# Two convolution layers with generated weights: wider statistics of x, an earlier start, first weights made beside the last loads, stores mixed with loads, last batch merged late

## The chip, the cores and the metric

The kernel runs on one core of one Trainium2 chip. The metric is the device time of one execution in microseconds. Several executions are timed in rounds against the kernel before on the same chip. No slow state showed in any run. A program on one core has a state only where several runs agree, so the two single runs (e2, e3) are of unknown state, and they are used for their profiles.

## The reference, cut to what matters

Two layers of the same form. Each normalizes x in 32 groups along the last axis, makes a convolution kernel of its own for each of 32 batches and 256 positions from a small network on z, applies it, and adds a bias and x itself.

```python
# x: (32 samples, 32 batches, 64 channels, 256 positions), float32
h = relu(layernorm(z @ W1 + b1))            # hidden layer, 128 wide
w = (h @ W2 + b2).reshape(B, L, CI, CO, 3)  # a kernel for each batch and position
bias = relu(layernorm(z @ Wb1 + bb1)) @ Wb2 + bb2
out = einsum('sbilk,bliok->sbol', x_unfolded, w) + bias
x = x + out(groupnorm(x))                   # twice, with weights of its own each time
```

The second layer's normalization needs statistics of the whole output of the first. The first needs those of the whole input.

## The kernel before

The kernel works in **units**: unit v is half the output channels of one batch, 64 units a layer. In a unit TensorE makes 12 weight groups (16 matmuls each, line 383 and 384), VectorE and ScalarE take them into the tile `wall`, and then the product (four blocks, line 426) multiplies the normalized x in `xn` with them. VectorE adds the residual (line 436) and, in layer 0, takes statistics of the result (line 228). GpSimd normalizes (line 373) and adds the bias (line 350). SyncE issues nearly all transfers in one order.

```python
gmean = const.tile([P, G, S], FP, name="gmean")
rstd = const.tile([P, G, S], FP, name="rstd")
parts = const.tile([P, GT, B, NH, 6], FP, name="parts")
prep = const.tile([P, 3, GT], FP, name="prep")       # 96 bytes a partition
...
w2 = big.tile([P, C, K * C], FP, name="w2t")
xn = big.tile([P, 2, M + 2, S], FP, name="xn")
room = big.tile([P, SH * L + RING * CH * LT], FP, name="room")
ys = room[:, S * M :].rearrange("p (r o l) -> p r o l", r=RING, l=LT)   # residual ring
```

```python
def store(v):                       # after the product of unit v
    u, h = divmod(v, NH)
    if u < B:
        nc.sync.dma_start(out=x1[u][h], in_=residual(v))       # 1 MB in 8 KB rows
        for t in range(NT):
            for a in range(2):                                 # 8 stores, runs of 128 bytes
                nc.sync.dma_start(
                    out=x1p[u][a * C + h * CH : a * C + (h + 1) * CH, :,
                               t * MT : (t + 1) * MT].rearrange("o s m -> s o m"),
                    in_=residual(v)[t * S : (t + 1) * S, :, a * MT : (a + 1) * MT])
...
def after(v):
    u, h = divmod(v, NH)
    if v >= 0:
        store(v)
    if v + 2 < NH * U:
        load_residual(v + 2)
    ...                             # hidden layer of a later batch
    if v + 1 == NH * B:             # between the layers
        stats()
        for k in range(2):
            next_pairs(B, k)        # normalize half a batch, load the next
    w, k = (u + 1, 1) if h == 0 else (u + 2, 0)
    if w != B:
        next_pairs(w, k)
    if v + 1 < NH * U:
        add_bias(v + 1)
    if v + 2 < NH * U:
        load_bias(v + 2)            # 4 loads of 256 KB
```

The opening (not shown) streams x once for its statistics, 256 elements an instruction, beside the 32 steps of the small network.

## Time and profile before

| | before |
|---|---|
| time, median of 3 runs | 4169.68 us (4168.51 to 4170.45) |
| profiled span | 4157.9 us (this execution took 4159.7 us, 10 less than the median) |
| first product starts | 319.7 us |
| layer 0, product 0 to product 61 | 1874.0 us, 30.7 us a unit |
| boundary, product 61 to product 66 | 188.5 us |
| product 66 to the end (layer 1) | 1775.7 us, 28.8 us a unit |

The page and the stretches of this kernel are read in the prediction below. Three more readings carry the argument after it. First, layer 0's loop from product 1 to product 61, sixty units (columns: stretch and length; busy time of PE, TensorE's matmuls, PEld, its weight loads, DVE, which is VectorE, ACT, which is ScalarE, and POOL, which is GpSimd, each with its instruction count; granted TensorE clock as a share of full speed; share of the DMA engines' time in use; GB/s):

```profile
349.70:2193.70 1844.00, 1747.98 (x42245) 1695.60 (x42245) 1211.18 (x1440) 560.64 (x1920) 920.69 (x180) 1.00 0.66 176
```

Second, the waits in that stretch (engine and line, what was waited for: us in total, times, longest us). "issue" is time in which the engine waited for nothing that the profile shows:

```profile
PE pc L426 <- issue: 81.8, 108, 2.4
```

Third, the same kind of line for layer 1, from product 67 on:

```profile
PE pc L426 <- issue: 12.2, 27, 0.9
```

So the products of layer 0 lose 82 us to waits without a visible reason, and those of layer 1 hardly any (12 us). Layer 1 has the same matmuls; it has neither the small-run stores nor the statistics. The page's DMA section lists an instruction queue, 709 packets and 11.62 MB (16.4 KB each). The "instruction blocks" of the prediction and of the expectations are these packets.

### The profile page before, as it was taken

The numbers are of one execution on the slowest core, as the hardware profiler recorded it, in microseconds if no ns is written. First come the engines' busy times: TensorE is split into PE (matmuls) and PEld (weight loads), VectorE is DVE, ScalarE is ACT, GpSimd is POOL, SyncE is SP. The second block draws the span as 40 slices with busy tenths as digits, with TensorE's granted clock in tenths as the row PEclk, the third lists the DMA queues.
The fourth block names the chain that finished last, engine by engine and source line by source line (L and its number), as shares of the span: only waits on it lengthen the run. The fifth ranks groups of instructions, "written<-read, shape, count | busy, mean of one in ns | idle before, by whom it ended". The sixth has DMA issues, their size and how long they took to land.

```text
span 4157.9 us, 194021 instructions
## 1 busy us (share of the span) xinstructions
PE 3917.2 (94%) x90704; PEld 3741.3 (90%) x90704; DVE 2642.2 (64%) x3168; ACT 1306.7 (31%) x4296; POOL 2078.0 (50%) x618
## 2 busy tenths in 40 slices
PE   5879999999999999999997899999999999999999
PEld 3449999999999999999997899999999999999998
DVE  6876666666666666666666465565655656555565
ACT  3433332322323323223232233333333333333332
POOL 3446544554554454454450744555445554455542
PEclk8669999999999999999999999999999999999999
DMA  8966676666666666667667354454444444444442
GB/s 316 343 247 186 172 188 160 179 186 170 182 169 176 187 163 181 177 170 186 164 176 208 125 163 153 144 167 131 160 150 145 163 131 162 150 148 159 135 153 88
DMA packets 655151, 718.51 MB, mean 173 GB/s; under 512 B 568516, under 2 KB 584968, under 8 KB 586248
## 3 DMA queue, kind: packets, MB, share of 16 engines
q1 hardware_dynamic: 628232, 692.46, 56.2%
q8 instruction: 709, 11.62, 1.2%
q10 hardware_dynamic: 26112, 13.64, 1.1%
q14 instruction: 98, 0.80, 0.1%
HBM read 492.08 MB, written 213.91 MB: 170 GB/s over the span
## 4 chain that ended last, share of the span: by engine, by line
PE 85%; DVE 6%; issue 3%; POOL 2%; DMA 2%; ACT 1%; ACTq 0%; SPq 0%; POOLq 0%; DVEq 0%
PE pg L383 54%; PE pc L426 23%; PE pg L384 7%; DVE wall L394 3%; POOL sq L182 1%; DVE parts L228 1%; DVE room L436 1%; DMA bd<-bs 1%; POOL xn L373 1%; ACT ht L200 0%; ACT sq L174 0%; PE p L170 0%; DMA spare<-in_xs_dram 0%; DMA xn<-in_xs_dram 0%; DMA room<-in_xs_dram 0%
## 5 line engine op out<-in xcount | busy, mean ns | idle before, releaser
L383 PE MATMUL pg<-hT,w2t 128*64 128x128 f32 x24576 | 2726.4, 273 | 13.6 <-DVE wall L394 9.4
L384 PE MATMUL pg<-hT,w2t 128*64 128x128 f32 x24576 | 2726.0, 273 | 1.9 <-issue 1.8
L383 PEld LDWEIGHTS pg<-hT,w2t 128*64 128x64 f32 x24576 | 2677.8, 137 | 36.9 <-DVE wall L394 22.9
L384 PEld LDWEIGHTS pg<-hT,w2t 128*64 128x64 f32 x24576 | 2678.0, 137 | 3.8 <-issue 3.8
L394 DVE TENSOR_TENSOR wall<-pg,b 128x1024 f32<-128x1024 f32 (+1 forms) x1536 | 1865.6, 1220 | 689.5 <-PE pg L384 685.9
L409 ACT ACTIVATE wall<-pg,b 64x128 f32<-64x128 f32 x4096 | 1189.1, 486 | 2640.8 <-DVE wall L394 2109.5
L373 POOL TENSOR_TENSOR xn<-room,gmean 128x2048 f32<-128x2048 f32 x128 | 605.8, 4733 | 1768.7 <-PE pc L426 1703.0
L426 PE MATMUL pc<-wall,xn 128*32 128x128 f32 (+2 forms) x40960 | 986.3, 253 | 122.9 <-issue 105.8
L426 PEld LDWEIGHTS pc<-wall,xn 128*32 128x32 f32 x40960 | 934.7, 110 | 181.2 <-issue 164.1
L436 DVE TENSOR_TENSOR room<-pc,room 128x512 f32<-128x512 f32 x512 | 354.2, 692 | 751.0 <-PE pc L426 629.2
L373 POOL TENSOR_TENSOR xn<-xn,rstd 128x2048 f32<-128x2048 f32 x128 | 786.5, 6145 | 10.0
L350 POOL TENSOR_TENSOR room<-room,bt 128x2048 f32<-128x2048 f32 x128 | 591.1, 4618 | 85.9 <-DMA bt<-bd 61.3
L228 DVE BATCH_NORM_STATS2 parts<-room 128x6 f32<-128x256 f32 x672 | 246.4, 416 | 8.7
L182 POOL TENSOR_TENSOR sq<-sq 128x512 f32<-128x512 f32 (+2 forms) x192 | 104.0, 541 | 150.9 <-ACT sq L174 138.4
L170 PE MATMUL p<-wc,zt 17*128 17x256 f32 x256 | 89.6, 506 | 36.5 <-DMA zt<-in_L_conv_z_dram 36.5
L170 PEld LDWEIGHTS p<-wc,zt 17*128 17x128 f32 x256 | 61.4, 252 | 57.1 <-DVE parts L228 32.7
L197 PEld LDWEIGHTS p<-ident,hs 128*128 128x128 f32 x256 | 49.9, 222 | 51.4 <-issue 51.4
L210 PE MATMUL p<-ht,Wb 128*64 128x512 f32 x64 | 59.3, 1027 | 31.5 <-ACT ht L200 31.5
L197 PE MATMUL p<-ident,hs 128*128 128x128 f32 x256 | 61.6, 421 | 3.7 <-DVE hs L188 3.7
L228 DVE BATCH_NORM_STATS2 parts<-xn 128x6 f32<-128x256 f32 x192 | 64.0, 408 | 0.0
L228 DVE BATCH_NORM_STATS2 parts<-spare 128x6 f32<-128x256 f32 x160 | 53.5, 411 | 0.0
L210 PEld LDWEIGHTS p<-ht,Wb 128*64 128x64 f32 x64 | 8.4, 185 | 47.4 <-ACT ht L200 44.5
(43 smaller groups left out, 232.0 us busy)
## 6 DMA issues: line engine op xcount, KB each, us to landing
bt<-bd SPq DMA_DIRECT2D x512, 256.0 KB, 8.3
room<-in_xp_dram SPq DMA_DIRECT2D x64, 1024.0 KB, 9.7
room<-in_xs_dram SPq DMA_DIRECT2D x64, 1024.0 KB, 5.8
x<-room SPq DMA_DIRECT2D x64, 1024.0 KB, 4.2
x1p<-room SPq DMA_DIRECT2D x512, 128.0 KB, 4.4
room<-x1p SPq DMA_DIRECT2D x64, 1024.0 KB, 8.9
room<-x SPq DMA_DIRECT2D x64, 1024.0 KB, 8.2
out_dram<-room SPq DMA_DIRECT2D x64, 1024.0 KB, 4.8
```

The lines of the kernel that those rows point to most:

```text
L170: nc.tensor.matmul(self.p1[:, k], self.zt[:, k * P : (k + 1) * P], self.t["wc"], start=True, stop=True)
L182: nc.gpsimd.tensor_tensor(to, self.sq[:, :, 0:w], self.sq[:, :, w : 2 * w], ALU.add)
L197: nc.tensor.transpose(p2[:, net, k * P : (k + 1) * P], hs[:, 2 * k + net, :], ident)
L228: nc.vector.bn_stats(out, y.rearrange("p o (a m) -> p o a m", a=2)[:, :, :, g * e : (g + 1) * e])
L350: nc.gpsimd.tensor_tensor(y, y, bts.pop(v), ALU.add)
L373: nc.gpsimd.tensor_tensor(o, i, b, op)
L383: nc.tensor.matmul(pg[0:C, k, :], w[:, k0 * C : (k0 + 1) * C], h0, start=True, stop=True)
L384: nc.tensor.matmul(pg[C:P, k, :], w[:, k1 * C : (k1 + 1) * C], h1, start=True, stop=True)
L394: nc.vector.tensor_tensor(place(rows, a), pg[rows].rearrange("p o (t m) -> p t m o", t=NT), b2[n][rows, kind, None, None, o0 : o0 + OG].to ...
L409: nc.scalar.activation(place(rows, 0)[:, :, :, k], pg[rows, k].rearrange("p (t m) -> p t m", t=NT), AF.Identity, bias=b2[n][rows, kind, o0 ...
L426: nc.tensor.matmul(pc[t * S : (t + 1) * S, n0 - q * EB : n1 - q * EB, :], xn[:, u % 2, t * MT + p + 1, :], wall[:, t, a : a + (n1 - n0) * CH],
L436: nc.vector.tensor_tensor(part, pc.rearrange("p (m a) o -> p o a m", a=2), part, ALU.add)
```

## The change

Its parts, by what they intend:

1. Statistics of x over 512 elements, so 256 instructions instead of 512.
2. The x stream first in the queue, layer 0's small weights on ScalarE's queue, the network's scratch moved into `xn`, so that `wall` can lie in the big pool and take x meanwhile.
3. Nine of the first unit's twelve weight groups made beside the last x chunks; the first normalizing on VectorE.
4. At the boundary, the first 31 batches' statistics reduced one unit early, the last batch merged in with small instructions; the bias before, other normalizing behind.
5. The eight small-run stores issued 2, 1 and 5 at a time between the loads.

```diff
+    wall = big.tile([P, NT, WT], FP, name="wall")
-    prep = const.tile([P, 3, GT], FP, name="prep")
+    first_parts = parts.rearrange(...)[:, 0 : GT * B * 6]
+    prep = const.tile([P, 6, GT], FP, name="prep")
 ...
+            small = [load_small(stage, layers[0], 0, nc.scalar)]
             made = {0: Hidden(stage, zts, small, 0)}
+            load(1)
+            load(2)
+            small.append(load_small(stage, layers[1], 1, nc.sync))
 ...
+                if i == first - 2:
+                    for k in range(NL):
+                        center(stage, small[k], k)
+                if i == (NQ - 2) * SQ:
+                    first_weights()
-                bn_stats(parts[:, g, u, h, :], xv[q % NX][:, j], g)
+                bn_stats(first_parts[:, g, u, 0, :], xu[q][:, j], g)
 ...
             if v + 1 == NH * B:
-                stats()
-                for k in range(2):
-                    next_pairs(B, k)
+                store_pairs(v, range(8))
+                last_batch()
+                diagonals()
+                return
+            store_pairs(v, range(2))
             w, k = (u + 1, 1) if h == 0 else (u + 2, 0)
             if w != B:
                 next_pairs(w, k)
+            store_pairs(v, range(2, 3))
             if v + 1 < NH * U:
-                add_bias(v + 1)
-            if v + 2 < NH * U:
-                load_bias(v + 2)
+                next_bias(v + 1)          # add_bias(v + 1), load_bias(v + 2)
+            if v + 2 == NH * B:
+                next_bias(v + 2)
+            store_pairs(v, range(3, 8))
+            if v + 1 == NH * (B - 1):
+                batches(parts, B - 1)
 ... (cut: reductions split up, normalize_first, main loop)
```

One line looks like bookkeeping: `prep` grows from 3 rows to 6 for the merging. It is a 96-byte tile that becomes 192 bytes, and every tile allocated behind it moves.

## The prediction

> **What bounds the kernel now.** I read the page first (engine totals, then the slices), then stretches by engine, then the timelines of the opening and of the boundary between the layers. The engine totals and one group, from the page:
>
> ```profile
> PE 3917.2 (94%) x90704; PEld 3741.3 (90%) x90704; DVE 2642.2 (64%) x3168; ACT 1306.7 (31%) x4296; POOL 2078.0 (50%) x618
> ...
> L228 DVE BATCH_NORM_STATS2 parts<-room 128x6 f32<-128x256 f32 x672 | 246.4, 416 | 8.7
> ```
>
> TensorE is the bound overall, so only the places where it stands idle or half idle can give time. The stretches: opening, loop of layer 0, boundary, loop of layer 1 (columns: stretch and length, busy time of PE, PEld, DVE, ACT, POOL, granted clock, DMA share, GB/s):
>
> ```profile
> 27.00:277.00 250.00, 205.32 (x576) 119.67 (x576) 210.67 (x570) 110.87 (x192) 110.44 (x224) 0.69 0.93 344
> 320.00:2262.00 1942.00, 1837.72 (x44412) 1782.86 (x44404) 1271.85 (x1512) 587.86 (x2016) 957.27 (x188) 1.00 0.67 178
> 2262.00:2327.00 65.00, 37.43 (x827) 32.77 (x820) 31.39 (x37) 12.24 (x35) 37.68 (x8) 0.84 0.42 125
> 2327.00:4144.00 1817.00, 1799.15 (x44180) 1773.48 (x44180) 1091.53 (x1007) 581.50 (x2016) 940.11 (x185) 1.00 0.46 148
> ```
>
> Layer 0's loop has 104 us of TensorE idle (1942 - 1838), layer 1's 18. The first product is at 319.75 us; until then everything is opening. In the opening DMA (93%), TensorE (82%) and VectorE (84%) are all nearly full. TensorE's timeline there, four of its 32 steps of the small network:
>
> ```profile
> 45.40 3.78 PE L170 MATMUL p<-wc,zt 17*128 17x256 f32 x8
> ...
> 81.36 1.99 PE L170 MATMUL p<-wc,zt 17*128 17x256 f32 x8
> 84.69 1.97 PE L210 MATMUL p<-ht,Wb 128*64 128x512 f32 x2 [1.34 <-ACT ht L200]
> 86.59 1.76 PE L197 MATMUL p<-ident,hs 128*128 128x128 f32 x8
> 88.27 1.99 PE L170 MATMUL p<-wc,zt 17*128 17x256 f32 x8
> ```
>
> A step takes 6.9 us (81.36 to 88.27) when the first matmuls take 1.99, because TensorE then waits for ScalarE, whose own round is Square 1.02, GpSimd's seven additions 3.93, Sqrt 0.3, two Relu 1.43: about 6.8. When they take 3.78 the step is 7.5. Over the opening the mean is 7.3 us (211 us for 29 steps). The small network is a bound of its own. VectorE's timeline at the start:
>
> ```profile
> 18.58 0.41 DVE L142 TENSOR_REDUCE wm<-wc 17x2 f32<-17x256 f32 x1 [17.57 <-DMA wc<-in_L_conv_Wb_dram]
> ...
> 25.31 7.21 DVE L228 BATCH_NORM_STATS2 parts<-xn 128x6 f32<-128x256 f32 x22
> ...
> 42.16 1.23 DVE L188 TENSOR_TENSOR hs<-p,var 128x1024 f32<-128x1024 f32 x1
> ```
>
> A weight of 8 KB issued at 5.8 us came at 18.5, just after the 4 MB load issued before it on the same queue (5.14 to 18.04).
>
> [...] its instruction queue has 709 packets and 11.62 MB, 16.4 KB each, and layer 0's chain shows products run in pieces of about 120 to 128 matmul records (each with its weight load) with waits called "issue" between. [...] the 22 statistics above come every 328 ns (7.21/22).
>
> **The change, part by part.**
>
> 1. Statistics over 512 elements. 512 instructions of 328 ns (168 us) become 256 [...], but VectorE isn't the sole bound, so little of it shows.
>
> 2. Start. The x load is first in the queue, in four pieces, so statistics start near 10 us instead of 25. But VectorE centers the weights of both layers after only six statistics, and layer 1's weights are issued on the sync queue behind loads 0, 1 and 2: 12.6 MB at 375 GB/s is 34 us, so they come at about 38 us. VectorE stands until then, then does ten statistics (6 us), and the first network scaling comes at about 45 us (before: 42.16). The early start is lost.
>
> 3. The network is squeezed into 13 of 16 chunks of statistics. It has 5.9 long statistics per step instead of 15 short ones (3.5 us against 5), but the step's round is ScalarE and GpSimd [...], neither changed. With somewhat less DMA crowding I take 7.1 us: the second scaling at 51, the last (thirty later) at 51 + 213 = 264 us (before: 268.7). Then 9 + 16 + 16 statistics remain before the last chunk (24 us), and that chunk's load must wait for the network's last stores out of the same buffer (about 13 us after the last scaling, and then 13 us for 4 MB): statistics end at 264 + 26 + 10 = 300, against 277.5 before. **This costs 22 us.**
>
> 4. After the statistics. Before, 42 us went from their end to the first product: eight reduction steps (11 us), diagonals and spreading (8), then 12 weight groups (21) beside GpSimd's 21.5 us of normalizing and 4.7 of bias. Now nine groups are made by ScalarE, 3 x 16 + 6 x 8 = 96 activations at 284 ns (2.27/8), 27 us, from when chunk 13 is done (280) to 308; the shorter reductions (512 instead of 1024 elements, about 4.5 us) end at 305 beside it. Then diagonals and spreading 7, three groups to 320.5, sixteen normalizing instructions [...] on VectorE (10): first product at about 330 against 319.75. **Opening: +11 us.**
>
> 5. Last batch merged. Before, from the end of the last layer 0 product (2271) to the first of layer 1 (2326.8) are 55.5 us, with reductions of 11 us, a stand before the spreading, and GpSimd doing two halves (21.5), the next batch's half (10.7) and the bias (4.5) in that order. Now the 31 batches are reduced one unit earlier, only eleven tiny instructions (2.2 us) remain, the bias is added before and the next batch's half after. Spreading ends about 13 us after the products, normalizing on GpSimd 22 us later: 35 us, 20 less. The early reduction (five of 1.5 us) stops the taking of weight groups in its unit and, with three PSUM buffers, costs TensorE about 7. **Boundary: -13 us.**
>
> 6. Loads and small-run stores interleaved. The same 0.52 million packets of 128 B move, but five of eight stores of a half batch go after the bias load, so the last 5 us before and into the products carry small packets instead of big loads. No engine waits for these loads now; what it may touch is the 1.4 us of "issue" per unit in layer 0 (64 x 1.4 = 90 us). [...] traffic reaching further into the products works the other way. Estimate: a fifth of it, **-18 us**, the least certain term.
>
> Sum: 4169.7 + 11 - 13 - 18 = 4150.
>
> **Rivals.** (a) The opening gains: if layer 1's weights came early, scaling would start near 20 us and every later step with it, making the opening -14 instead of +11, total 4125. For: the change plainly intends it. Against: the 18.5 us landing above. (b) Instruction waits grow: stores now run to about 25 us after the start of a unit of 31 us, and the products start at 21; if a block waits as it did beside the last weight loads at 2264 us (2.9 us of issue), a unit loses 1 us more, total 4230. For: that wait; against: those were big packets. (c) The interleaving removes most issue waits: layer 0's unit falls from 31.0 to near 29.5, total 4080.
>
> **Range and chances.** The opening is good to 10 us either way, the boundary to 6, the loop to 30: together about 35. The change looks tuned, which shifts some weight to the fast side. I say 4150, 4100 to 4195, and faster by over 2% (under 4086) needs rival (c), or (a) and half of (c).
>
> **What would show it.** VectorE standing until about 38 us after six statistics, waiting for wc; last scaling near 264; statistics ending near 300 with the load into xn waiting on the network's stores; first product near 330; 35 us from the last layer 0 product to the first of layer 1, and a hole of about 7 us one unit before; layer 0's unit near 30.7 us with less issue. Layer 1 must be unchanged (28.85 us a unit). Wrong would be a changed clock in the loops, or a new wait of GpSimd for late loads in layer 0.

## The result, and the profile after

| | before | after |
|---|---|---|
| time, median of 4 runs each | 4169.1 us (4165.33 to 4170.45) | 4181.04 us (4178.19 to 4187.87) |
| ratio after to before | | 1.0032 (95%: 1.0015 to 1.005) |

A ratio is the mean time of one kernel's fast runs over that of the other's of the same rounds, so it is not quite the ratio of the medians. The change makes the kernel 0.3% slower, where a gain of 0.5% had been predicted. The two profiles, by where each unit's product starts:

| stretch | before | after | difference | predicted |
|---|---|---|---|---|
| start to product 0 | 319.7 | 342.1 | +22.3 | +11 |
| product 0 to 61 | 1874.0 | 1878.8 | +4.8 | -18 |
| product 61 to 66 | 188.5 | 178.9 | -9.6 | -13 |
| product 66 to end | 1775.7 | 1778.1 | +2.4 | 0 |
| span | 4157.9 | 4177.9 | +20.0 | -20 |

Single profiles scatter, so small differences in this table mean little. The profiled execution of before is a fast one: the spans differ by 20 us, the timed medians by 12. Over all runs below, the six profiles with the opening of before (before, f1, f4, f5, h1, h2) start product 0 between 319.7 and 323.7 us, and the six with the changed opening (after, e1, e2, e3, f2, f3) between 342.1 and 348.1 us. Two pairs with the same layer 0 (before and e5, changed and e4) differ by 5 and 7 us from product 1 to product 61.

From the page of the changed kernel, the engine totals and the statistics of those ten x chunks that lie in `wall`:

```profile
PE 3923.3 (94%) x90704; PEld 3746.7 (90%) x90704; DVE 2622.5 (63%) x2926; ACT 1325.8 (32%) x4384; POOL 2038.6 (49%) x628
...
L246 DVE BATCH_NORM_STATS2 parts<-wall 128x6 f32<-128x512 f32 x160 | 97.3, 677 | 7.8 <-DMA beb<-in_L_conv_beb_dram 7.8
```

TensorE has the same 90704 matmuls and is busy 6 us longer. VectorE is 20 us lighter, which buys nothing. VectorE's timeline in the opening (start, length, engine, line, operation, output and input, count, and in brackets the idle time before and what ended it):

```profile
8.80 3.66 DVE L246 BATCH_NORM_STATS2 parts<-wall 128x6 f32<-128x512 f32 x6 [7.79 <-DMA beb<-in_L_conv_beb_dram]
...
36.58 0.41 DVE L159 TENSOR_REDUCE wm<-wc 17x2 f32<-17x256 f32 x1 [23.18 <-DMA wc<-in_L_conv_Wb_dram]
...
43.77 1.23 DVE L207 TENSOR_TENSOR xn<-p,var 128x1024 f32<-128x1024 f32 x1
```

Statistics start at 8.8 us instead of 25.3, but after six of them VectorE stands 23 us for layer 1's weights, and the first scaling of the network comes at 43.8, later than the 42.2 of before. The end of the opening, first before:

```profile
269.84 7.60 DVE L228 BATCH_NORM_STATS2 parts<-xn 128x6 f32<-128x256 f32 x23
277.47 1.50 DVE L296 TENSOR_REDUCE prep<-parts 128x8 f32<-128x1024 f32 x1
```

and after:

```profile
272.37 14.91 DVE L246 BATCH_NORM_STATS2 parts<-wall 128x6 f32<-128x512 f32 x25
287.20 9.58 DVE L246 BATCH_NORM_STATS2 parts<-room 128x6 f32<-128x512 f32 x16
297.04 9.59 DVE L246 BATCH_NORM_STATS2 parts<-xn 128x6 f32<-128x512 f32 x16 [0.26 <-DMA xn<-in_xs_dram]
306.66 0.83 DVE L340 TENSOR_REDUCE prep<-parts 128x8 f32<-128x512 f32 x1
...
321.35 1.22 DVE L471 TENSOR_TENSOR wall<-pg,b 64x1024 f32<-64x1024 f32 x1 [8.31 <-PE pg L460]
...
325.99 1.02 DVE L446 TENSOR_TENSOR xn<-room,gmean 128x512 f32<-128x512 f32 x1
```

After the network's last scaling VectorE still has 57 long statistics to do (25, 16 and 16, 34 us in a row), where before 23 short ones were left (7.6 us). So they finish at 306.6 us instead of 277.5. The load into `xn`, which the network's scratch holds until its end, lands at the same moment as VectorE gets to it: VectorE waits 0.26 us for it. Layer 0's loop from product 1 to product 61, and its waits:

```profile
374.10:2220.90 1846.80, 1751.98 (x42242) 1695.61 (x42240) 1211.08 (x1440) 558.04 (x1920) 910.41 (x181) 1.00 0.72 176
```

```profile
PE pc L505 <- issue: 82.2, 123, 2.7
```

A loop of the same length, within the scatter, with the same waits: the stores' new order seems to do nothing. That is the main puzzle, since it was the largest gain that the prediction named. At the boundary, the early reduction (five instructions of 1.5 us in a row) stands before the taking of the weight groups, and step 61 to 62 grows from 30.6 to 39.0 us:

```profile
2232.28 1.20 DVE L471 TENSOR_TENSOR wall<-pg,b 64x1024 f32<-64x1024 f32 x1
2233.40 1.48 DVE L340 TENSOR_REDUCE prep<-parts 128x8 f32<-128x992 f32 x1
...
2241.12 3.47 DVE L471 TENSOR_TENSOR wall<-pg,b 128x1024 f32<-128x1024 f32 x3
```

### The profile page after: what moved, and what is told of

It reads as the page before. It is cut to its first block, busy times and chain, and to the rows that moved or that the text cites. A ratio compares the mean times of both kernels' runs of the same rounds, so it can differ in the third digit from the quotient of the medians.

```text
span 4177.9 us, 193861 instructions
## 1 busy us (share of the span) xinstructions
PE 3923.3 (94%) x90704; PEld 3746.7 (90%) x90704; DVE 2622.5 (63%) x2926; ACT 1325.8 (32%) x4384; POOL 2038.6 (49%) x628
## 4 chain that ended last, share of the span: by engine, by line
PE 84%; DVE 6%; issue 3%; DMA 2%; POOL 2%; ACT 1%; ACTq 0%; POOLq 0%; DVEq 0%; SPq 0%
PE pg L459 54%; PE pc L505 24%; PE pg L460 5%; DVE wall L471 3%; POOL xn L201 2%; DVE parts L246 1%; DVE room L515 1%; DMA hd<-xn 1%; ACT xn L218 1%; DMA zt<-in_L_conv_z_dram 1%; ACT xn L193 1%; POOL xn L446 1%; PE p L190 0%; DMA wc<-in_L_conv_Wb_dram 0%; DVE xn L446 0%
## 5 line engine op out<-in xcount | busy, mean ns | idle before, releaser
L471 DVE TENSOR_TENSOR wall<-pg,b 64x1024 f32<-64x1024 f32 x1527 | 1854.3, 1220 | 679.2 <-PE pg L460 675.2
L436 POOL TENSOR_TENSOR xn<-room,gmean 128x2048 f32<-128x2048 f32 x124 | 581.8, 4692 | 1751.5 <-PE pc L505 1719.2
L436 POOL TENSOR_TENSOR xn<-xn,rstd 128x2048 f32<-128x2048 f32 x124 | 746.8, 6022 | 9.7
L246 DVE BATCH_NORM_STATS2 parts<-room 128x6 f32<-128x256 f32 (+1 forms) x592 | 241.6, 454 | 8.7
L201 POOL TENSOR_TENSOR xn<-xn 128x512 f32<-128x512 f32 (+2 forms) x192 | 104.1, 542 | 154.3 <-ACT xn L193 141.7
L190 PE MATMUL p<-wc,zt 17*128 17x256 f32 x256 | 88.4, 500 | 28.9 <-DMA zt<-in_L_conv_z_dram 28.9
L216 PEld LDWEIGHTS p<-ident,xn 128*128 128x128 f32 x256 | 50.0, 223 | 63.4 <-issue 63.4
L246 DVE BATCH_NORM_STATS2 parts<-wall 128x6 f32<-128x512 f32 x160 | 97.3, 677 | 7.8 <-DMA beb<-in_L_conv_beb_dram 7.8
L228 PE MATMUL p<-xn,Wb 128*64 128x512 f32 x64 | 55.2, 960 | 31.2 <-ACT xn L218 31.2
L216 PE MATMUL p<-ident,xn 128*128 128x128 f32 x256 | 61.9, 422 | 18.2 <-DVE xn L207 18.2
```

The source lines that it names most:

```text
L190: nc.tensor.matmul(self.p1[:, k], self.zt[:, k * P : (k + 1) * P], self.t["wc"], start=True, stop=True)
L201: nc.gpsimd.tensor_tensor(to, self.sq[:, :, 0:w], self.sq[:, :, w : 2 * w], ALU.add)
L216: nc.tensor.transpose(p2[:, net, k * P : (k + 1) * P], hs[:, 2 * k + net, :], ident)
L246: nc.vector.bn_stats(out, y.rearrange("p o (a m) -> p o a m", a=2)[:, :, :, g * e : (g + 1) * e])
L436: nc.gpsimd.tensor_tensor(o, i, b, op)
L471: nc.vector.tensor_tensor(place(rows, a), pg[rows].rearrange("p o (t m) -> p t m o", t=NT), b2[n][rows, kind, None, None, o0 : o0 + OG].to ...
```

## The experiments

"Loop" below is always product 1 to product 61, sixty units, in the profiled run: 1844.0 us before, 1846.8 after.

### What the order of the stores is worth: e1

The changed kernel with its eight small-run stores together, directly behind the store of x1, as before.

```diff
             store(v)
+            if v + 1 != NH * B:
+                store_pairs(v, range(8))
 ...
-            store_pairs(v, range(2))  / range(2, 3) / range(3, 8)
```

> The changed kernel with the eight small-run stores of a half batch together again, right after the long store, as before. Theory A (the order of these stores and loads is worth nothing, since no engine waits for these loads and the issue waits of TensorE were 81.8 us before and 82.2 us after): layer 0's unit stays at 30.8 us (30.78 in the changed kernel, 30.73 before), the whole within 6 us of 4181. Rival B (the interleaving does help, and another part of the change costs the loop what it gives): a unit of 31.1 us or more, the whole 20 us longer. Rival C (interleaving hurts): a unit of 30.5 or less, the whole 20 us shorter.

Measured: correct, 4239.66 us (4236.2 to 4243.31, 4 runs), ratio to before 1.0165 (1.0148 to 1.0181). Its loop, and its waits:

```profile
376.70:2282.60 1905.90, 1763.28 (x42244) 1713.83 (x42242) 1210.72 (x1440) 558.14 (x1920) 905.79 (x180) 0.99 0.67 170
```

```profile
PE pc L505 <- issue: 131.0, 102, 3.3
```

So interleaving takes 59 us off the changed kernel's loop (1905.9 - 1846.8), three times the predicted 18. Then something else in the change must put 62 us on: e1 has the store order of the kernel before and its loop is 1905.9 against 1844.0. All of it shows on TensorE: 49 us more of issue waits in the products and 15 us more of busy time.

### What puts 60 us on the loop: f1, f2, f3, f4, f5

The addresses in the built programs gave the suspicion. Behind `prep` every tile is 96 bytes later in the changed kernel: `room` starts at byte 106752 before, a multiple of 256, and at 106848 after. The small-run stores read the residual in `room` in pieces of 128 bytes. Before, these start at 0 or 128 modulo 256; after, at 96 or 224, and the second kind crosses a 256-byte line (an address that is a multiple of 256). That such a crossing costs time was a guess of the author's at this point; f1 and f5 test it.

**f1**: the kernel before, shifted and nothing else.

```diff
-    prep = const.tile([P, 3, GT], FP, name="prep")
+    prep = const.tile([P, 6, GT], FP, name="prep")
```

> The kernel before with one number changed: the small constant tile prep has 6 rows instead of 3, as in the changed kernel, so that every SBUF tile behind it, room with the residual ring among them, starts 96 bytes later. In the kernel before room starts at byte 106752, a multiple of 256; here at 106848. Theory A (the missing 63 us of the layer 0 loop come from that shift: the 128-byte pieces of the residual that the small-run stores read now straddle 256-byte lines): 4230 us (4215 to 4245), the loop from unit 0 to unit 61 at 1935 us instead of 1874, issue waits of TensorE near 130 us instead of 82. Rival B (the shift does nothing; the place of the weight wall or the order of the opening is to blame): 4170 us, loop 1874.

Measured: correct, 4226.47 us (4219.72 to 4229.51, 4 runs), ratio 1.0131 (1.0113 to 1.0148).

```profile
351.90:2252.60 1900.70, 1760.23 (x42243) 1710.28 (x42243) 1210.18 (x1440) 557.68 (x1920) 905.75 (x180) 0.99 0.67 171
```

```profile
PE pc L426 <- issue: 126.8, 106, 2.9
```

One number in a small constant tile costs 57 us of loop (1900.7 - 1844.0): 45 us of issue waits and 12 us of busy time. Theory A, as far as this run goes, holds.

The 12 us have a likely cause in the trace, easily passed over (the 0.99 in the line above). Its clock records show ten stretches of 3.4 us at half clock in this loop, each after 2.0 to 2.6 us of TensorE idleness within the 3.4 us before; matmuls in them take 367 to 406 ns on average instead of some 270. By estimate, half speed for ten times 3.4 us can cost up to 17 us. e1's loop has twelve such stretches, that of before and that of the changed kernel none, e5 and f5 three each. So long waits may cost more than their own length here. No run tests this apart, and busy time also moves without it: in h1 below it falls by 15 us at an unchanged clock.

**f2**: the changed kernel with `prep` at 11 rows, so that all offsets modulo 256 are those of before.

> The changed kernel with prep at 11 rows, so that everything behind it lies on the same offsets modulo 256 bytes as in the kernel before. Theory A: the loop gets back about 60 us: 4120 us (4105 to 4140), loop 1820 instead of 1879. Rival B: 4181 us, loop 1879.

Measured: correct, 4180.51 us (13 runs), ratio 1.0016 (1.0007 to 1.0024), loop 1846.1. **A miss**: with the stores interleaved, putting the addresses right gives next to nothing (the changed kernel has a ratio of 1.0032, 1.0015 to 1.005). Its waits, 82.2 us in the changed kernel:

```profile
PE pc L505 <- issue: 77.7, 117, 3.0
```

**f3**: e1 with `prep` at 11 rows.

> The changed kernel with its eight small-run stores together as in the kernel before (e1) and prep at 11 rows. Theory A: the loop is the one of the kernel before, 1876 us, and the whole 4240 - 61 = 4179 us (4170 to 4190). Rival B: 4240 us, loop 1937.

Measured: correct, 4189.35 us (6 runs), ratio 1.0046 (1.0031 to 1.0061), loop 1853.4. With e1's 1905.9 this is the shift again, 52 us, now taken off the changed kernel.

**f4**: the kernel before with the stores issued 2, 1 and 5 at a time, addresses as they were.

> The kernel before with nothing changed but the order of the stores: the eight small-run stores issued 2, 1 and 5 at a time between the loads, as in the changed kernel; addresses as before. If interleaving is worth the same 58 us here as between e1 and the changed kernel: 4112 us (4095 to 4130), loop 1816. Rival C (interleaving only helps where the short pieces are out of line): 4160 to 4172 us. My prediction's own figure for this part was 18 us: 4152.

Measured: correct, 4164.23 us (20 runs), ratio 0.9984 (0.9975 to 0.9992), loop 1845.8. Its loop and its waits:

```profile
354.10:2199.90 1845.80, 1755.81 (x42241) 1697.53 (x42240) 1210.61 (x1440) 560.68 (x1920) 922.77 (x181) 1.00 0.71 176
```

```profile
PE pc L429 <- issue: 76.9, 124, 3.0
```

The second **miss** of the theory that the two effects add, and what rival C said: interleaving helps much where the pieces are out of line. Elsewhere it is worth 7 to 9 us of time (0.16% of 4173.5 here; f2's median is 8.8 below f3's), and this profile's loop, against the fast one of before, shows none of it.

**f5**: a control, the kernel before shifted by 128 bytes instead of 96.

```diff
-    prep = const.tile([P, 3, GT], FP, name="prep")
+    prep = const.tile([P, 7, GT], FP, name="prep")
```

> Control of f1: the kernel before with prep at 7 rows instead of 3, so that everything behind it moves by 128 bytes instead of 96. The 128-byte pieces of the residual then start at 128 or 0 modulo 256 and none crosses a 256-byte line, where in f1 every second one (224 to 352) did. If crossing the line is the cost: as the kernel before, 4172 us (4160 to 4182), the 128-byte packets at 12.8 ns. If any displacement of the tiles from their 256-byte places costs it, or the larger constant tile does: 4226 us as f1, packets at 14.3 ns.

Measured: correct, 4175.51 us (20 runs), ratio 1.001 (1.0002 to 1.0019). The tile is larger and everything has moved further than in f1, and the time is that of before but for some 4 us. Its loop is 15 us longer than that of before, with these waits:

```profile
PE pc L426 <- issue: 95.4, 109, 2.6
```

That is a quarter of f1's 57 us and more than the 4 us of the timed runs; part of it is the fast profile of before, the rest is open. So nearly all of f1's cost comes from the crossing of the line and not from the displacement. The loops side by side:

| loop, us | pieces inside a line | pieces crossing a line |
|---|---|---|
| stores together | 1844.0 (before), 1853.4 (f3), 1859.2 (f5) | 1900.7 (f1), 1905.9 (e1) |
| stores interleaved | 1845.8 (f4), 1846.1 (f2) | 1846.8 (after) |

Three of the four fields are alike within 15 us. The change moved along the diagonal: its fifth part pays for what its `prep` rows do, and little is left over. The trace's records of DMA packets show the shift directly. Mean time of the 128-byte packets in the loop, all of them, then by the kind of store (worked out from the records of product 1 to product 61; the eight stores of a unit are told apart by order of start, which overlap blurs a little, and which can't be done where they are interleaved):

```
                              all      first half of a row   second half
before                        12.8 ns       12.6 ns            13.1 ns
f1, shifted by 96 bytes       14.3 ns       12.7 ns            16.0 ns
f3, together, aligned         12.8 ns       12.5 ns            13.1 ns
e1, together, shifted         14.3 ns       12.7 ns            16.0 ns
f5, shifted by 128 bytes      12.8 ns       12.5 ns            13.1 ns
f4, interleaved               14.0 ns
f2, interleaved, aligned      14.1 ns
after, interleaved, shifted   14.5 ns
```

With the stores together only the pieces that cross the line got slower, 16.0 against 13.1 ns (the 8 KB packets of the loop take 411 ns in f1, 408 before). In sum this is 0.77 us a unit of all 16 engines (8192 packets x 1.5 ns / 16), and the unit grew by 0.95 us (57 / 60). With the stores interleaved all small packets are slower, and the shift adds only 0.4 ns to each (14.5 against 14.1), 0.2 us a unit. So one reason why the new order hides the shift may be that there is less of it to hide.

### Why a unit waits, and why the order hides the shift: e2, e3, h1, h2

**e2**: the same bytes to x1p in runs of 4 KB (wrong result on purpose), in the changed kernel.

```diff
-                    out=x1p[u][a * C + h * CH : ..., :, t * MT : (t + 1) * MT]...,
+                    out=<the same number of bytes of x1p[u], contiguous>,
```

> The changed kernel with the same bytes stored to the pair tensor in runs of 4 KB instead of 128 B, to wrong places (a wrong result on purpose). Theory A (layer 0's products wait for instruction blocks because much DMA traffic runs beside them): the small packets go, the DMA share of layer 0 falls from 0.72 to about 0.5, the issue wait of 82 us in 60 units falls below 30, and the unit falls from 30.8 towards layer 1's 28.9. Theory B (layer 0's longer products come from VectorE's statistics between the products and not from DMA): the DMA share falls all the same, and the unit stays above 30.5.

Measured: 4137.72 us (one run, state unknown). From product 1 to 61 a unit takes 30.16 us (1809.8 / 60) instead of 30.78. Between 410 and 2186 us:

```profile
410.00:2186.00 1776.00, 1717.44 (x41534) 1666.73 (x41532) 1190.41 (x1417) 547.20 (x1888) 890.44 (x177) 1.00 0.56 180
```

```profile
PE pc L505 <- issue: 45.0, 84, 1.0
```

Theory A is right in direction, and only half in size: it asked for waits below 30 us and a unit towards 28.9.

**e3**: no statistics of layer 0's outputs (wrong result on purpose), a tiny memset instead of each.

> The changed kernel without statistics of layer 0's outputs: each is replaced by a memset of its 6 results (a wrong result on purpose). Per unit that takes 8 x 0.375 = 3.0 us from VectorE between the products. Theory A (DMA delays instruction blocks): issue waits stay near 1.35 us a unit and the unit falls by at most 0.4 us, to 30.4. Theory B (VectorE's round per product block, 1.77 us against TensorE's 1.8, with two PSUM buffers, makes the waits): the issue waits go and the unit falls to about 29.2.

Measured: 4163.31 us (one run, state unknown), a unit 30.56 us (1833.4 / 60); the issue waits between 410 and 2180 us are 85.5 us. So VectorE's statistics cost a unit some 0.2 us, and the issue waits stay without them.

What are these waits? In the loop of before, TensorE has 138 stands of over 0.2 us. Of these, 133 end 1 to 3 us after the end of a 16 KB packet of the instruction queue, the median 1.41 us, though such packets come only every 5.6 us. So they are read here as waits for instructions. When in a unit they come, and what the DMA engines do then, is in the trace too. Stands of TensorE of over 0.1 us, in us a unit, by the time since the product's start:

```
us into the product      0-2    2-4    4-6    6-9
before                   0.00   0.88   0.03   0.49
f1 (shifted)             0.00   1.67   0.00   0.49
f4 (interleaved)         0.07   0.42   0.29   0.48
after (both)             0.06   0.52   0.28   0.48
e2 (long runs)           0.01   0.27   0.14   0.36
before, layer 1          0.00   0.00   0.06   0.22
```

And the share of the 16 DMA engines' time in use, in steps of 2 us from the product's start (packet times of product 1 to product 61, summed):

```
us into the product      0-2    2-4    4-6    6-8    8-10   10-12
before                   0.58   0.07   0.03   0.01   0.03   0.55    nearly all 8 KB packets
f1 (shifted)             0.88   0.20   0.02   0.02   0.02   0.19    nearly all 8 KB packets
f4 (interleaved)         0.97   0.48   0.14   0.03   0.03   0.56    nearly all 128 B packets
after (both)             0.99   0.50   0.17   0.03   0.03   0.54    nearly all 128 B packets
e2 (long runs)           0.40   0.04   0.04   0.01   0.07   0.83    mostly 4 KB packets
```

(The notes at the right are for the first 4 us.) A unit's transfers begin when its product ends and nearly fill the DMA engines from then on: in before, 0.80 to 1.06 of their time in each step of 2 us from 12 to 30 us (packet times summed, so a step can pass 1). They just about fill the 21 us until the next product and run over into its start. There TensorE loses most (0.88 us a unit at 2 to 4 us in before). A shift of 0.8 us a unit lengthens this overrun of big packets, and the waits 2 to 4 us into the product double (0.88 to 1.67 us). With the stores interleaved the overrun is made of small packets, is longer (0.48 and 0.50 of the engines' time at 2 to 4 us), and hurts less there (0.42 and 0.52 us) but also later (0.29 and 0.28 us at 4 to 6 us); why small packets hurt less was not tried. This makes a theory: the overrun is what TensorE pays for. h1 and h2 test it.

**h1**: the kernel before, with three of the four bias loads of each unit left out after the first (wrong result on purpose). The small packets stay.

```diff
-            for t in range(NT):
+            for t in range(NT if v == 0 else 1):      # into one bias tile kept throughout
```

> The kernel before with three of the four bias loads of each unit left out after the first (wrong result on purpose): 0.75 MB a unit less, at the end of the unit's burst; the 8192 small packets a unit are as before. Theory A (the burst's overrun into the next product delays the instruction fetches): the overrun goes, the 0.9 us a unit of waits 2 to 4 us into the product go with it, issue waits of the loop fall from 82 to some 30 us, loop 1785 to 1800 instead of 1844. Rival B (the small packets hold TensorE up wherever they run): loop 1835 to 1845.

Measured: wrong as intended, 4078.45 us (2 runs), ratio 0.9785 (0.9738 to 0.9832).

```profile
351.70:2117.30 1765.60, 1733.07 (x42246) 1692.09 (x42244) 1210.69 (x1440) 560.62 (x1920) 923.49 (x180) 1.00 0.57 157
```

```profile
PE pc L428 <- issue: 21.0, 37, 1.0
```

The overrun is gone (0.02 of the engines' time in the first 8 us), and so are the waits 2 to 4 us into the product (0.04 us). The loop falls by 78 us, more than the 44 to 59 expected: 61 us of issue waits and 15 of busy time. h1 also moves less, 157 GB/s against 176; but e2, at 180 GB/s, had fewer waits too, so the amount alone doesn't set them.

**h2**: h1 with `prep` at 6 rows.

> h1 with prep at 6 rows, so with the 96-byte shift of the changed kernel (wrong result on purpose). Theory A: the small packets take 12% longer, 0.8 us a unit, but the burst now ends before the product all the same: loop within 12 us of h1's, where the shift alone cost 57 us. Rival B: 45 to 57 us above h1.

Measured: wrong as intended, 4080.53 us (2 runs), ratio 0.979 (0.975 to 0.9831), loop 1767.6:

```profile
352.90:2120.50 1767.60, 1733.22 (x42245) 1691.85 (x42242) 1211.13 (x1440) 556.81 (x1920) 912.43 (x180) 1.00 0.59 157
```

```profile
PE pc L428 <- issue: 23.4, 38, 1.1
```

The small packets again take 14.3 ns instead of 12.9, and now this costs 2 us of loop instead of 57. That settles this part: the shift makes each small packet that crosses a line slower (16.0 ns against 13.1, f1 and before), and in this kernel TensorE pays for it only where the burst has no room left before the next product. How a running transfer delays the instruction packet is not shown by these runs: the packet itself takes no longer (1.12 us before, 1.07 us in f1).

### The opening: e4, e5

**e4**: the changed kernel with layer 1's weights centered only when they are needed.

```diff
                 if i == first - 2:
-                    for k in range(NL):
-                        center(stage, small[k], k)
+                    center(stage, small[0], 0)
+                if i == 6 * SQ:
+                    center(stage, small[1], 1)
```

> The changed kernel with layer 1's small weights centred at the start of chunk 6, not after six statistics, so that VectorE doesn't wait 23.2 us for a load queued behind 12 MB. Theory A (the small network is the bound of the opening and starts late because of this wait): first scaling at about 20 us instead of 43.5, last scaling about 23 us earlier (248 instead of 271), first product near 319 instead of 342, the whole 4181 - 23 = 4158. Rival B (the DMA stream of x bounds the opening as it did before, 93% busy): the network starts early and is then held by late chunks; the last scaling comes at 262 or later and the whole at 4170 or more.

Measured: correct, 4173.68 us (12 runs), ratio to before 1.0000 (0.9992 to 1.0009). The first scaling comes at 24.96 us instead of 43.77, 18.8 us earlier, but the last at 261.5 instead of 271.2, and the first product at 332.3 instead of 342.1: 10 us earlier each. That is near what rival B said (262 or later, 4170 us or more) and far from theory A (248, 4158 us). One wait took most of the other half, ScalarE's until 76.3 us for a store of the network, issued at 60.6 us while two x loads of 4 MB, issued at 51.5 and 52.6 us, were under way:

```profile
76.33 0.78 ACT L218 ACTIVATE xn<-p,be,g 128x512 f32<-128x512 f32 x1 [9.34 <-DMA hd<-xn]
```

**e5**: the kernel before with the wider statistics of x alone.

> The kernel before with one part of the change alone: the statistics of x over 512 elements in 256 instructions instead of 256 elements in 512, all else as before. My prediction's theory: the opening is paced by the hidden chain (32 links of some 7.3 us), so VectorE's 27 us less work buys nothing but a few us at the tail: first product 312 to 320 us against 319.7, whole 4164 to 4173. Rival (VectorE's work stretches the links of the chain): first product below 305, whole below 4160.

Measured: correct, 4163.19 us (19 runs), ratio 0.998 (0.9972 to 0.9987), first product 318.9 us against 319.7 (322.1 to 323.7 in the five other profiles with the opening of before, so the work saved may be worth up to 5 us). The rival, a first product below 305, is out. Its last scaling is at 275.2 us, where the kernel before has 268.7 and the changed one 271.2: the network's 32 links came later, which took back most of what the shorter stretch after them gained (43.7 us to the first product, 51.0 before). Where the 0.2% of time come from, about 8 us, these profiles don't show.

### A better version: g1, g2, k1, k2, k3

**g1**: the opening and addresses of before (`prep` at 11 rows), the interleaved stores, the merged last batch, and the eight early operations of the merging spread one behind each weight group.

```diff
                 take(pg, n, kind, o0)
+                if v == NH * (B - 1) and k > 0:
+                    for piece in early[k - 1 : k]:
+                        piece()
```

> The kernel before with its own opening and addresses (all tiles on the offsets modulo 256 they had), the interleaved stores and the merged last batch of the change, and the eight early operations of that merging spread one after each weight group instead of in one row. Sum from the runs: opening 320 as before, loop 1844 to 1847 as before, boundary (unit 61 to unit 66) 188.5 before, 178.9 in the changed kernel, less 4 to 8 for the hole of 8.4 us that the spreading fills: 171 to 175. Whole: 4173 - 9 (interleaving alone, f4) - 10 (merging) - 5 (spreading) = 4149 us (4138 to 4160). Rival (the runs' parts don't add: what the boundary gains is given back in the loop or layer 1): 4160 to 4170.

Measured: correct, 4154.08 us (4147.8 to 4158.32, 5 runs), ratio 0.9958 (0.9943 to 0.9973). Loop 1842.3, boundary 175.4 (188.5 before, 178.9 in the changed kernel). The parts add up as expected, but for the hole: step 61 to 62 is 36.6 us instead of 39.0, so spreading filled 2.4 of 8.4 us. The last piece, on 8 elements, shows 3.84 us instead of the 0.17 in the changed kernel; why was not tried.

**g2**: g1 with three of the eight groups of the boundary's normalizing moved from GpSimd to VectorE, behind its last weight group.

> g1 with the normalizing of the boundary shared: GpSimd does five of the eight groups at once, VectorE the last three behind its last weight group. GpSimd's 16 operations took 22.9 us in the changed kernel and product 64 ran 18.4 us beside them instead of 7.5. If that wait sets the boundary: 6 to 9 us below g1, product 64 under 12 us. Rival (the weight groups ahead of product 64 set it): as g1 within 3 us.

Measured: correct, **4150.05 us** (4149.08 to 4151.05, 4 runs) against 4170.85 of before in the same rounds, ratio 0.9953 (0.9938 to 0.9968). Boundary 173.7 us, product 64 16.2 us instead of 18.5: the sharing brings less than expected, as its rival said. This is the fastest correct version by ratio, 0.5% faster than before and so faster than both kernels; its interval overlaps with those of g1 and of k3 below.

**k1, k2, k3**: g2 with one load of the unit moved into the 6 us in which the DMA engines idle beside the product (0.01 to 0.03 of their time in use from 4 to 10 us into it, before): the residual of unit v+2 is released after block 2 of product v (k1), after block 1 (k2), and after block 2 with the stores together (k3).

```diff
                     for g in range(2 * q, 2 * q + 2):
                         bn_stats(parts[:, g, u, h, :], y, g)
+                    if q == 2:
+                        nc.vector.memset(residual(v + 2)[:, 0, 0:1], 0.0)
+                        load_residual(v + 2)
```

> g2 with the load of the residual of unit v+2 (1 MB) released after the third of the four blocks of product v, through a memset of one column by VectorE, instead of after product v's last store: some 3 us of the unit's DMA work then lie in the 6 us in which the engines idled. If the burst's overrun is what costs the loop its waits: the loop falls from 1841 by 40 to 60 us, whole 4095 to 4115. Rival (traffic beside the rest of the product delays its fetches as much, or VectorE's memset waits for the late stores of unit v-1): loop 1825 to 1850, whole 4140 to 4160.

> k1 with the release one block earlier, after the second block. More of the load lies in the idle time, but nearer to the fetches that the product needs in its first 8 us, and nearer to the late stores of the unit before. Theory: within 15 us of k1. Rival: 20 to 40 us above k1, with waits 4 to 8 us into the product.

> k1 with the eight small-run stores together, as in the kernel before, so that they have all landed by the time of the memset. Theory: without an overrun the order of the stores doesn't matter: within 12 us of k1, whole 4095 to 4115. Rival (interleaving has a worth of its own): 20 us or more above k1.

Measured: all correct; 4150.19 (20 runs), 4144.07 (8) and 4141.12 us (4), on a chip where before has 4161.34; ratios 0.9976 (0.9968 to 0.9983), 0.9972 (0.9955 to 0.9989) and 0.9962 (0.9947 to 0.9977). Loops 1852.8, 1837.9 and 1840.9. **Misses**: none gained the 40 to 60 us, and by ratio none is better than g2 (0.9953, 0.9938 to 0.9968). The trace shows that the overrun mostly stayed (k3's products still lose 54.5 us to issue waits between 400 and 2100 us), because the last loads of a unit are gated by other things. In odd units the bias load waits until GpSimd's bias addition has freed the bias tile (in a unit of k3 that I followed it is issued 25 us into the unit); in even ones the interleaved stores still come last. In k2 it vanished behind every second unit, and the products there took 8.3 us, the others 9.1; but stands of 0.37 us a unit came up 11 us into the unit. So the harm of the overrun shows inside this one kernel too, and a version that gets rid of it with a right result remains to be found.

## Why the prediction was wrong, point by point

- **Loop of layer 0 (step 6, -18 us): this step failed, and it is the largest error.** The step took "a fifth" of 90 us of issue waits, by the author's estimate; no run had then shown that interleaving shortens them. Measured: waits of 82.2 us against 81.8, and a loop of +2.8 us (1846.8 - 1844.0), or +4.8 with the first unit. Two things were wrong. First, the size: on aligned addresses interleaving takes 5 to 14 us of waits (f4: 76.9 against 81.8; f2: 77.7 against f3's 91.7) and 7 to 9 us of time. Second, the prediction read the `prep` line as storage only, and so missed that it shifts the residual by 96 bytes (f1: +57 us with the stores together; f5: +4 us of time for 128 bytes). Interleaving hides this shift (e1 to after: -59 us). The shift is not what kept the 18 us away: with it undone the changed kernel has the same loop (f2: 1846.1). Right in its reasoning was that traffic reaching into the product makes the issue waits longer (21.0 us in h1, 23.4 in h2, 81.8 before); that these are waits for instruction blocks fits the packet times (133 of 138 stands end 1 to 3 us after the end of such a packet). It didn't see that this overrun makes most of them: 61 of 82 us go with it (h1).
- **Rivals (b) and (c): out.** The waits didn't grow, and layer 0's unit is 30.78 us (30.73 before).
- **Opening (steps 2 to 4, +11 us): right in kind, half the size, +22.3.** Step 2 holds: VectorE stood until 36.6 us after six statistics, first scaling 43.8 (said 45; its 375 GB/s is what before moved from 25 to 50 us). Step 3's link of 7.1 us was mis-sized: 7.34 us ((271.2 - 43.8) / 31; the parts of the round that the prediction adds to "about 6.8" make 6.7), so the last scaling came at 271 instead of 264. From there to the end of the statistics it said 36 us and measured 35.4, so these ended at 306.6 instead of 300; but it was VectorE's 57 statistics that filled the time, and the wait for the load into `xn` was 0.26 us. In step 4 the normalizing instructions take 1.02 us each, 16 of them 16.3 us, where the author's estimate was 10. The rest of the gap is passed on from the late statistics: the three groups end at 326 instead of 320.5. Rival (a), that early weights would give 25 us, is out: e4 came 10 us earlier.
- **Step 1 held.** 512 elements take 0.61 us (3.66 / 6; the author's estimate was 6 us for ten), and e5 shows that the work saved is worth little there (0.8 us against the profile of before).
- **Boundary (step 5, -13 us): right, -9.6.** The hole of the early reduction is 8.4 us, said 7, and without it the boundary gained 18, said 20. Its way there was less exact: the 55.5 us that it read from before run to the second half of product 64, whose first half starts at 2311.6 us, 39.7 us after product 63. In the changed kernel this gap is 36.5 us, said 35. After that the wait moved to GpSimd's normalizing beside product 64, which runs 18.4 us.
- **Layer 1 unchanged: right**, +2.4 us in one profile.
- **The sum.** Of the 40 us between the forecast span and the profiled one, the loop is 23, the opening 11, the boundary 3 and layer 1 2. The range (4100 to 4195) held the result; the sign was wrong. That the result stayed so near is luck in part: the shift that nobody foresaw costs 57 us by itself, and the interleaving happened to hide it.

## What to carry to other kernels

Look at what a change does to addresses: a constant tile that grows by 96 bytes moved every tile behind it, and where DMA reads them in 128-byte pieces, every second piece crossed a 256-byte line and took 16.0 ns instead of 13.1 (f1). Compare the addresses before judging any other part. Before changing the order of transfers, see when in the loop the engine that bounds it stands and which transfers run then: here, transfers that ended before the next product cost next to nothing (h2: 2 us), and what ran over cost TensorE up to 57 us (f1). And take a change apart in both directions, from the kernel before and from the kernel after: here the shift costs 57 us with the stores together and nothing that shows with them interleaved, and either direction alone would have missed that.
